# Issuing the small adapter loads of block 0 on two queues behind the first piece of x

## The chip, the cores and the metric

The kernel runs on one core of one Trainium2 chip. The metric is the device time of one execution in microseconds, a median over several runs.

## What is computed

The input x has 8 sequences of 256 tokens with 1024 features. Each sequence picks one of eight low-rank adapters (rank 16) by an id that is known only when the program runs. The adapted tokens go through a gated feed-forward layer with fp8 rounding of its inputs, and the result is added to x:

```python
Bx  = einsum('bni,bri->bnr', x, B[ids])          # B: 8 x 16 x 1024
h   = einsum('bnr,bor->bno', Bx, A[ids])         # A: 8 x 1024 x 16
gate, up = q(h / s_g) @ Wg.T, q(h / s_u) @ Wu.T  # 1024 -> 2752, q rounds to fp8
hid = silu(gate) * up
out = x + q(hid / s_d) @ Wd.T                    # 2752 -> 1024
```

## The kernel before

The 2048 tokens are four blocks of 512, of two sequences each, and the 2752 hidden features are 22 chunks of 128 (the last is half full). TensorE does everything in one long sequence whose order is written out by hand (`multiply`, L469, keeps program order; all its matmuls carry the line number L470). It starts with matmuls on zeros (`warm`, L633). Then, for block 0, come B (`two_times_b`, tile bx: eight steps over the features, k = 0 to 7), A (`two_times_a`, tile c, rounded to fp8 into xg), and the gate and up matmuls of the first five weight chunks (tile y). Blocks 1 to 3 take their turns among the first chunks. The other chunks follow for all blocks, and then the down projection (tile yd).

All loads go through queues of DMA transfers. Most are issued by SyncE (SP), one after the other in the order of the program. Two are issued by ScalarE (ACT): the ids, and one half of B. A load whose address depends on an id needs that id in a register of the issuing engine: `adapter_of` (L362) loads it there from the tile ids_i.

For block 0 the loads are these:

- x in three pieces, of which the first has k = 0 to 3 (1 MB), the second k = 4 to 6 (0.75 MB), the third k = 7 (0.25 MB); `load_x(0, 0)`, `load_x(0, 4)` and `load_x(0, 7)`.
- B for its two sequences (`load_b`, 68 KB each). B's tile also carries the scales. The k-th step of bx needs B and that k of x.
- A for its two sequences (`load_a_two`, two loads of 32 KB for each, into rows of a tile that POOL has set to zero, L357). The first matmul to tile c needs all four.
- the weights of the first five chunks (`load_gate_up`, 1 MB each; chunk 0 in two halves). The y matmuls need them in that order.

The scheduler gives each load one of eight landing semaphores, in turn and in the order of the program, and a load that reuses a semaphore is issued only after the earlier load on it has landed. In the kernel before, the turns are: ids, x's first piece, B and B, x's second piece, and three of the four A loads; then the fourth A load (waits for the ids), x's third piece (waits for x's first piece), chunk 0's halves (wait for the two B loads), chunk 1 (waits for x's second piece), and the others.

Of the kernel before, what the change touches and what calls it, by code (L numbers as in the profile page):

```python
# [59 lines left out]
def x_of(x4, t, k):  # L60

    first = 0
    for n in PIECES[t]:
        if k < first + n:
            break
        first += n
    at = (t * NH + first) * P * TB
    piece = x4[at : at + n * P * TB].rearrange("(p k n) -> p k n", p=P, k=n)
    return piece, first
# [214 lines left out]
def adaln_ffn(  # L284
# [13 lines left out]
    nc = tc.nc  # L298
# [38 lines left out]
    with ExitStack() as fast:  # L337
# [14 lines left out]
        b_two = [lora.tile([P, 2 * BROW + R], F32, name=f"b{t}") for t in range(2)]  # L352
# [9 lines left out]
        def adapter_of(batch, queue):  # L362
            return queue.value_load(ids_i[0:1, batch : batch + 1], min_val=0, max_val=7)  # L363

        def load_b(b, i, adapter, queue):
            queue.dma_start(  # L366
                out=b[:, i * BROW : (i + 1) * BROW], in_=b8[bass.ds(adapter * P, P), :]
            )

        def load_a_two(t, j, adapter):  # L370
            for g in range(2):
                row = 32 * (2 * g + j) + R * j
                nc.sync.dma_start(
                    out=a_two[t][row : row + R],
                    in_=a8[bass.ds(adapter * 2 * R + g * R, R), :],
                )

        def load_x(t, k):
            piece, first = x_of(x4, t, k)
            ks = slice(first, first + piece.shape[1])  # L380
            nc.sync.dma_start(out=xs[t][:, ks, :], in_=piece)
# [9 lines left out]
                nc.sync.dma_start(out=w[:, bass.ts(i, n)], in_=src[:, bass.ts(i, n)])  # L391
            w_of[c] = w

        load_x(0, 0)
        load_b(b_two[0], 0, adapter_of(0, nc.scalar), nc.scalar)
        second = adapter_of(1, nc.sync)
        load_b(b_two[0], 1, second, nc.sync)


        load_x(0, 4)  # L400
        load_a_two(0, 1, second)
        load_a_two(0, 0, adapter_of(0, nc.sync))
        load_x(0, 7)
        for c in range(NFIRST):
            load_gate_up(c, parts=1 if c else 2)
# [5 lines left out]
        for j in range(2):  # L411
            load_a_two(1, j, adapters.pop(0))
# [317 lines left out]
        for k in range(NH - 1):  # L730
# [23 lines left out]
            first = k % 2 == 0  # L754
# [29 lines left out]
    with found_others.Else():  # L784
# [11 lines left out]
        t, cols = NTB - 1, slice(cut, TB)  # L796
# [88 lines left out]
```

## Time and profile before

| what | value |
|---|---|
| median of 3 runs | 476.82 us (476.09 to 476.93) |
| the profiled execution | 477.12 us |
| its span, first to last instruction | 475.3 us |
| TensorE matmuls busy | 469.8 us, 99% of the span |
| granted TensorE clock | 1.0 |
| DMA, mean over the span | 112 GB/s |
| x's first piece, issue to landing | 5.0 us |
| the two halves of B, issue to landing | 3.2 and 3.3 us |
| x's third piece, issue to landing | 2.9 us |

Times in the views are counted from the span's first instruction. A line of the timeline gives start, length, engine, line of the kernel, operation, the tiles written and read, how many instructions were merged, and in brackets how long the engine was idle before it and what ended that. An engine's name with a q (SPq, ACTq) stands for what its queue issues. "DMA x<-x" in the chain is a transfer from its issue to its landing.

### The profile page before, as it was taken

What the parts mean: (1) busy time and instruction counts of PE and PEld (TensorE: products, weight loads), DVE (VectorE), ACT (ScalarE), POOL (GpSimd) and SP (SyncE); (2) the same over time, 40 slices, a digit from 0 to 9 for tenths busy, and PEclk for the clock granted to TensorE, in tenths of its full rate; (3) what the DMA queues carried; (4) which work ended last, traced back from release to release, by engine and by line L of the source; (5) the groups of instructions that cost most, each with busy time, mean ns of one, the idle gap of its engine ahead of it and who ended that gap; (6) DMA issues with size and microseconds to landing.
All of it is one profiled execution on the core that took longest, in us unless ns stands there. A gap on an engine that the chain in (4) does not pass through costs nothing.

```text
span 475.3 us, 6009 instructions
## 1 busy us (share of the span) xinstructions
PE 469.8 (99%) x2514; PEld 217.0 (46%) x2514; DVE 105.6 (22%) x163; ACT 192.5 (40%) x249; POOL 1.0 (0%) x7
## 2 busy tenths in 40 slices
PE   8999999999999999999999999999999999999997
PEld 4454544444444444444444444444444444444444
DVE  1333432121212222121212212132120121031031
ACT  1322447995556654533454554359212022021000
POOL 0000000000000000000000000000000000000000
PEclk9999999999999999999999999999999999999999
DMA  8995013422222112222211111123335255063031
GB/s 291 406 405 186 1 48 133 176 88 90 88 88 89 24 66 89 90 88 88 90 30 60 44 62 56 61 83 123 103 146 161 64 185 161 22 213 114 3 116 66
DMA packets 13780, 53.44 MB, mean 112 GB/s; under 512 B 1650, under 2 KB 2930, under 8 KB 10674
## 3 DMA queue, kind: packets, MB, share of 16 engines
q1 hardware_dynamic: 13600, 52.92, 32.1%
q8 instruction: 21, 0.34, 0.3%
q14 instruction: 13, 0.11, 0.1%
q10 hardware_dynamic: 146, 0.07, 0.0%
HBM read 44.60 MB, written 8.39 MB: 111 GB/s over the span
## 4 chain that ended last, share of the span: by engine, by line
PE 96%; DMA 3%; SPq 0%; issue 0%; DVE 0%
PE y L470 62%; PE yd L470 31%; DMA w_gu<-w_gu 2%; PE c L470 1%; PE bx L470 1%; DMA x<-x 1%; DMA ids_i<-ids 0%; SPq L363 0%; SPq L366 0%; DVE o L695 0%; PE count L470 0%
## 5 line engine op out<-in xcount | busy, mean ns | idle before, releaser
L470 PE MATMUL y<-xg,w_gu 128*128 128x512 fp8e4 x1376 | 298.4, 379 | 0.9 <-DMA w_gu<-w_gu 0.9
L470 PEld LDWEIGHTS <-w_gu 128*128 128x128 bf16 x1376 | 134.0, 98 | 163.8 <-DMA w_gu<-w_gu 1.8
L470 PE MATMUL yd<-hid,w_d 128*128 128x512 fp8e4 (+2 forms) x693 | 146.0, 373 | 0.0
L609 ACT ACTIVATE g<-y,gate_s 128x512 f32<-128x512 f32 (+1 forms) x88 | 59.8, 681 | 137.2 <-PE y L470 137.2
L610 DVE SCALAR_TENSOR_TENSOR hid<-y,up_by_down,g 128x512 fp8e4<-128x512 f32 x84 | 63.1, 751 | 220.3 <-PE y L470 162.2
L470 PEld LDWEIGHTS <-w_d 128*128 128x128 bf16 x693 | 66.6, 98 | 79.0 <-issue 1.7
L456 ACT ACTIVATE junk<-w_d 128x1408 bf16<-128x1408 uint16 (+1 forms) x16 | 21.2, 1324 | 88.4 <-DMA w_d<-w_d 88.3
L695 DVE SCALAR_TENSOR_TENSOR o<-yd,down_s,x 128x512 f32<-128x512 f32 x28 | 20.0, 748 | 107.4 <-PE yd L470 92.8
L456 ACT ACTIVATE junk<-w_gu 128x2048 bf16<-128x2048 uint16 (+1 forms) x22 | 41.0, 1863 | 0.0
L463 ACT ACTIVATE junk<-hid 128x2048 bf16<-128x2048 fp8e4 x21 | 40.0, 1905 | 0.4
L463 ACT ACTIVATE junk<-xg 128x2048 bf16<-128x2048 fp8e4 x8 | 15.3, 1909 | 0.3
L528 ACT ACTIVATE xg<-c,inv 128x512 fp8e4<-128x512 f32 x16 | 9.7, 688 | 8.6 <-PE c L470 8.6
L526 DVE TENSOR_SCALAR xg<-c,inv 128x512 fp8e4<-128x512 f32 x16 | 10.9, 744 | 2.8 <-PE c L470 2.8
L470 PE MATMUL warm<-zeros 128*128 128x512 bf16 (+1 forms) x27 | 6.5, 402 | 1.2 <-DVE zeros L309 1.2
L695 DVE SCALAR_TENSOR_TENSOR o<-yd,down_s,xg 128x512 f32<-128x512 f32 (+2 forms) x5 | 3.2, 644 | 12.3 <-PE yd L470 12.3
L516 ACT COPY bm<-bx 64x128 f32<-64x128 f32 x4 | 1.0, 262 | 9.7 <-PE bx L470 9.6
L470 PE MATMUL bx<-x,b 128*32 128x128 f32 x128 | 4.3, 276 | 0.6 <-DMA x<-x 0.6
L470 PEld LDWEIGHTS <-zeros 128*128 128x128 bf16 x27 | 2.6, 116 | 4.7 <-issue 3.0
L470 PE MATMUL c<-bm,a 32*128 32x128 f32 x128 | 4.3, 277 | 0.0
L456 ACT ACTIVATION_READ_ACCUMULATOR junk<-w_gu 128x1 f32 x22 | 4.2, 191 | 0.0
L470 PEld LDWEIGHTS c<-bm,a 32*128 32x128 f32 x128 | 3.9, 186 | 0.5 <-ACT bm L516 0.4
L470 PE MATMUL yd<-hid_tail,w_dt 64*128 64x512 bf16 (+1 forms) x32 | 4.1, 377 | 0.0
(47 smaller groups left out, 41.0 us busy)
## 6 DMA issues: line engine op xcount, KB each, us to landing
w_gu<-w_gu SPq DMA_DIRECT2D x20, 1024.0 KB, 4.8
outT<-o SPq DMA_DIRECT2D x31, 256.0 KB, 2.2
w_d<-w_d SPq DMA_DIRECT2D x8, 704.0 KB, 4.8
w_d<-w_d SPq DMA_DIRECT2D x8, 640.0 KB, 3.9
x<-x SPq DMA_DIRECT2D x2, 2048.0 KB, 11.1
x<-x SPq DMA_DIRECT2D x2, 1024.0 KB, 8.6
x<-x SPq DMA_DIRECT2D x2, 768.0 KB, 9.5
w_gu<-w_gu SPq DMA_DIRECT2D x3, 512.0 KB, 3.8
```

What stands on the lines that cost most here:

```text
L456: nc.scalar.activation(junk_like(w), low(w), AF.Copy, accum_out=lows[:rows, column : column + 1])
L463: nc.scalar.activation(junk_like(q), q, AF.Square, accum_out=squares[:rows, column : column + 1])
L470: tc.keep_in_program_order(nc.tensor.matmul(*args, **kwargs))
L516: copy(bm[64 * to : 64 * (to + 1), other], bx[half][64 * half : 64 * (half + 1)],)
L526: nc.vector.tensor_scalar(to, c, scale, None, ALU.mult, saturate=False)
L528: nc.scalar.activation(to, c, AF.Copy, scale=scale, saturate=False)
L609: nc.scalar.activation(g[rows], gates, AF.Silu, scale=gate_s[: gates.shape[0]])
L610: nc.vector.scalar_tensor_tensor(to, in0=ups, scalar=up_by_down[rows], in1=g[rows], op0=ALU.mult, op1=ALU.mult, saturate=False,)
L695: nc.vector.scalar_tensor_tensor(o, in0=y, scalar=down_s, in1=x, op0=ALU.mult, op1=ALU.add)
```

## The change

The four A loads of block 0 move ahead of x's second piece, and the two of the first sequence are issued by ACT, behind the half of B that ACT issues already. SP no longer loads the first sequence's id, since ACT has it in a register. The order on SP becomes: x's first piece, B, two A loads, x's second piece, x's third piece, weights. The order on ACT: ids, B, two A loads. In the turns of the semaphores the four A loads now come fifth to eighth, x's second piece reuses that of the ids, x's third piece that of x's first piece as before, and chunk 1 that of an A load.

```diff
-        def load_a_two(t, j, adapter):
+        def load_a_two(t, j, adapter, queue=nc.sync):
             for g in range(2):
                 row = 32 * (2 * g + j) + R * j
-                nc.sync.dma_start(
+                queue.dma_start(
                     out=a_two[t][row : row + R],
                     in_=a8[bass.ds(adapter * 2 * R + g * R, R), :],
                 )
...
         load_x(0, 0)
-        load_b(b_two[0], 0, adapter_of(0, nc.scalar), nc.scalar)
-        second = adapter_of(1, nc.sync)
+        first, second = adapter_of(0, nc.scalar), adapter_of(1, nc.sync)
+        load_b(b_two[0], 0, first, nc.scalar)
         load_b(b_two[0], 1, second, nc.sync)
-
-
+        load_a_two(0, 0, first, nc.scalar)
+        load_a_two(0, 1, second)
         load_x(0, 4)
-        load_a_two(0, 1, second)
-        load_a_two(0, 0, adapter_of(0, nc.sync))
         load_x(0, 7)
```

## The prediction on record

> **What bounds the kernel now.** I read the page first: busy shares, then the chain that ended last.
>
> ```profile
> PE 469.8 (99%) x2514; PEld 217.0 (46%) x2514; DVE 105.6 (22%) x163; ACT 192.5 (40%) x249; POOL 1.0 (0%) x7
> PE 96%; DMA 3%; SPq 0%; issue 0%; DVE 0%
> ```
>
> TensorE is the bound for 96% of the chain, and the change touches no matmul. Only the 3% under DMA can move. So I asked for the chain in order of time, to see where that part lies (start, length, what).
>
> ```profile
> 2.92 0.37 SPq L366
> 3.29 0.04 issue
> 3.33 4.97 DMA x<-x
> 8.30 0.02 issue
> 8.32 8.85 DMA w_gu<-w_gu
> 17.17 0.05 issue
> 17.21 13.12 PE y L470 x60
> ```
>
> The last DMA on the chain is the weights of chunk 1, landed at 17.17 us. From 17.21 on the chain holds nothing but TensorE up to the last eviction, so the kernel ends 458 us after that landing, whatever came before. The question is therefore one number: when does chunk 1 land? Third, the timeline of the first 18 us (start, length, instruction, idle before it).
>
> ```profile
> 2.88 0.41 ACTq L366 DMA_DIRECT2D b<-b  x1
> 2.92 0.37 SPq L366 DMA_DIRECT2D b<-b  x1
> 3.33 0.45 SPq L381 DMA_DIRECT2D x<-x  x1
> 4.00 2.58 SPq L373 DMA_DIRECT2D a<-a  x4
> 6.62 0.42 SPq L381 DMA_DIRECT2D x<-x  x1
> 7.09 2.99 SPq L391 DMA_DIRECT2D w_gu<-w_gu  x6
> 8.34 0.86 PE L470 MATMUL bx<-x,b 128*32 128x128 f32 x24 [0.22 <-DMA x<-x]
> 9.59 0.43 PE L470 MATMUL bx<-x,b 128*32 128x128 f32 x8 [0.38 <-DMA x<-x]
> 14.70 1.90 PE L470 MATMUL y<-xg,w_gu 128*128 128x512 fp8e4 x8 [0.23 <-DMA w_gu<-w_gu]
> 17.21 13.12 PE L470 MATMUL y<-xg,w_gu 128*128 128x512 fp8e4 x60 [0.62 <-DMA w_gu<-w_gu]
> ```
>
> SyncE (SP) spends 2.58 us on the four A loads, and x's third piece is issued only after them, at 6.62. TensorE waits four times for data, 0.22 + 0.38 + 0.23 + 0.62 = 1.45 us in all; 0.85 of it is for weights. Fourth, the DMA's rate in stretches (the last column is GB/s, the one before it the share of the 16 engines).
>
> ```profile
> 5.00:5.50 0.50, 0.50 (x3) 0.25 (x2) 0.00 (x0) 0.00 (x0) 0.00 (x0) 1.00 1.14 380
> 7.00:7.50 0.50, 0.50 (x29) 0.50 (x20) 0.00 (x0) 0.00 (x0) 0.00 (x0) 1.00 0.95 373
> 7.50:8.00 0.50, 0.50 (x16) 0.25 (x8) 0.00 (x0) 0.00 (x0) 0.00 (x0) 1.00 0.89 176
> 8.00:8.50 0.50, 0.28 (x11) 0.16 (x12) 0.00 (x0) 0.00 (x0) 0.00 (x0) 1.00 0.52 160
> 8.50:9.00 0.50, 0.50 (x24) 0.44 (x16) 0.00 (x0) 0.00 (x0) 0.00 (x0) 1.00 1.19 426
> ```
>
> Around 400 GB/s is normal here; between 7.5 and 8.5 the stream runs at 176 and 160. The loss is 0.5 x (1 - 176/400) + 0.5 x (1 - 160/400) = 0.58 us of transfer time. It is the stretch in which x's second piece is done and the third, issued at 6.62, has not begun to flow. I call it the hole.
>
> **What the Trainium skill says.** (1) "DMA: Bandwidth & Descriptors", section "Issuing engines are not separate DMA queues": loads from ACT and SP share the same 16 engines, and a second issuing queue saves only issue time. This decides what to count: not a second stream, but SP's 2.58 us. The trace agrees as far as it goes: B's two halves, issued at 2.88 on ACT and 2.92 on SP, took 3.2 and 3.3 us to land. (2) Same page, "Queues, rings and completion order": on each engine a queue's descriptors are consumed in ring order, and an engine drains a packet before it turns to another queue. The trace agrees: B on ACT's otherwise empty queue landed at 6.08, after x's first piece (issued 0.75, 5.0 us to landing, so 5.75). (3) Same page, "Latency and other measured facts": first byte about 0.6 us after the issue. Here the measurement decides: x's third piece was issued at 6.62, and the rate is back only after 8.1, so 1.5 us from issue to flow.
>
> **The change part by part.** Nothing is added or taken away in computing. One register load of batch 0's adapter (0.28 us with 0.16 us of register arithmetic behind it) goes from SP; ACT already holds that register.
>
> *ACT's side.* Two A loads follow B on ACT, at about 3.5 and 4.1 us by SP's pitch (4.00 to 4.59 for the first two A loads). ACT's next work is the copy at 10.11 us, which waits for TensorE until then: cost zero, and the cover is 5 us thick. Both A tiles' zeroing (0.53 us from 1.02 on POOL) is long done.
>
> *SP's side.* B ends at 3.29. Before, the first A came 0.22 us after its predecessor's end, so now at 3.51, the second 0.59 us later at 4.10, ending 4.43. x's second piece is issued at 4.47, 1.14 us later than the 3.33 of before. The third piece could go at 4.96, but in the compiled order it reuses the landing semaphore of x's first piece (eight in rotation), so it waits for 5.75 and goes at 5.77, 0.85 us earlier than 6.62. The weights follow at 6.24 instead of 7.09; their own semaphores belong to B (6.08 and 6.22) and to A, all landed by about 6.7. Queued behind that wait on SP are only weight loads, and the stream has x's second piece to move meanwhile.
>
> *The hole of before.* x's second piece, issued 4.47, flows from about 4.47 + 1.5 = 5.97. Its 0.79 MB take 1.97 us at 400 GB/s, to 7.94. The third piece is ready at 5.77 + 1.5 = 7.27: it follows without a gap. The hole closes: -0.58 us.
>
> *A new hole?* x's first piece landed at 5.75; its last byte moved earlier. x's third piece flowed from 8.1 for 0.65 us and landed at 9.52, 0.77 later; so the first was through between 5.0 and, with no such delay on most engines, 5.5. I take 5.25. B's 0.139 MB and A's 0.131 MB now lie between it and the second piece: 0.27/0.4 = 0.67 us, to 5.92. The second piece is ready at 5.97. Bounds: with 1.0 us to flow it is there at 5.47 and there is no hole; with 2.1 us, which would be the case if it behaves as B did (3.2 us to landing less some 1.1 for arriving), it is there at 6.57 and leaves 0.65 us. I take 1.5, as measured for the third piece of x, and 0.08 us for a ragged change. Net for the stream: 0.58 - 0.08 = 0.5 us earlier.
>
> *TensorE's side.* The first bx group starts at 6.71 behind the warm-up matmuls, which end at 6.78; x's first piece (5.75) and B (6.08, 6.22) have half a microsecond to spare, so it stays. x's second piece lands 0.35 us later (A is now ahead of it), 8.65 instead of 8.30, so the 24 matmuls run 8.65 to 9.51. The third piece lands at 7.94 + 1.3 = 9.2, in time; the last eight start at 9.51 instead of 9.59. Everything to the first y follows: 12.50 instead of 12.58. Two groups of eight (1.89 and 1.90) end at 16.29 if chunk 0's second half is there at 14.39; it lands at 14.65 - 0.5 = 14.15. Chunk 1 lands at 17.17 - 0.5 = 16.67, later than 16.29, so DMA still ends last and the whole 0.5 us counts. Late next would be TensorE itself at 16.29: a gain beyond 0.92 us is closed. After that, loads that came 0.5 us earlier meet a TensorE that is 0.5 us earlier too.
>
> Sum: the profiled execution goes from 475.3 to about 474.8 of span, 477.12 to about 476.6 with the 1.8 us around it. The median shown, 476.82, lies 0.3 below that execution; I apply the 0.5 to it: 476.3.
>
> **The rivals.** *The hole only moves* (18%). The second piece of x needs 2.1 us to flow, a hole of 0.65 at 6 us replaces that of 0.58 at 8 us: 476.82 + 0.07 = 476.9. For it: the second piece is issued 1.14 us later. Against it: 0.27 MB of B and A fill just that time.
>
> *The lag of the last share, longer: slower* (17%). Chunk 0's first half landed at 10.9 (7.09 + 3.8), its second only at 14.65, 3.75 us later, while the stream moved about 1.4 MB and the half has 0.52. At the rates there (336, then 397 GB/s) 1.4 us would do, so the last share of it came 2.3 us behind the rest, and chunk 1 behind it. Place: the first weights, 11 to 15 us, beside the fp32 matmuls. The two queues' small loads shift what meets there. Price: the lag's growth less 0.5, so it decides above 0.5 us of growth. Nothing shows its size; between no growth and doubling I take 1.5: 477.8. Against it: the same weights come in the same order.
>
> *The lag goes* (15%). Chunk 1 is then early, and TensorE's 16.29 is the limit: 0.92 us, 475.9.
>
> That the change does not do what it says is excluded: the compiled order has the loads so.
>
> **How the numbers follow.** The forecast has 50%, by itself 475.9 to 476.8. A difference of 0.2% (0.95 us) is about what a measurement of this kernel can tell; the three runs lie 0.84 us apart. Faster by that: about half of the vanished lag and a tenth of the forecast, 0.13. Slower: six tenths of the longer lag and a little of the moved hole, 0.13. Within: 0.74. The range, 475.6 to 477.7, leaves out half of the longer lag and a quarter of the vanished one.
>
> **What would show it.** Right: third piece of x issued near 5.8, weights near 6.2; no stretch under 300 GB/s between 7 and 9; second piece of x landed near 8.65; the y group behind chunk 1 starting near 16.7. Wrong: a stretch under 250 GB/s between 5.5 and 6.5 (the hole moved); chunk 1 later than 17.2 with the stream full (the lag); the first bx group later than 6.8 (B late); or a change after 20 us, where I expect none.

## The result, and the profile after

The changed kernel takes 478.04 us (median of 20 runs, 477.19 to 479.6), the kernel before 476.88 (median of 20, 475.71 to 478.39). The ratio is 1.0024, with a 95% interval of 1.0014 to 1.0035: slower by 0.24%, or 1.16 us. The forecast was 476.3, with a range up to 477.7. It failed in sign.

The runs of the changed kernel fall into two groups. In 11 of the 20 the mean granted TensorE clock is 0.999 or 1.0, and their median is 477.38. In the other 9 it is 0.996, and their median is 478.79. The profiled execution is one of the quick ones: 477.19 us, the least of the 20, with a span of 475.4. The profiled execution of before (477.12) was slower than its median. So the two spans, 475.3 and 475.4, hide the difference, and the stages have to be compared instead.

First the chain that ended last in the changed kernel, in order of time (start, length, what):

```profile
4.42 0.04 issue
4.47 5.68 DMA x<-x
10.14 0.04 issue
10.19 1.09 PE bx L470 x32
11.28 0.50 PE warm L470 x7
11.77 2.10 PE c L470 x63
13.88 16.52 PE y L470 x76
```

The weights are gone from the chain. The last data that anything waits for is x's second piece. It is issued at 4.47, as the prediction worked out, but lands at 10.15, not at 8.65. Everything after it is TensorE without a gap. The timeline of the same kernel shows the wait (in the brackets) and the issues:

```profile
3.48 0.95 ACTq L373 DMA_DIRECT2D a<-a  x2
3.52 0.91 SPq L373 DMA_DIRECT2D a<-a  x2
4.47 1.46 SPq L381 DMA_DIRECT2D x<-x  x2
6.12 3.11 SPq L391 DMA_DIRECT2D w_gu<-w_gu  x6
8.71 0.40 PE L470 MATMUL warm<-zeros 128*128 128x128 bf16 x4
10.19 1.09 PE L470 MATMUL bx<-x,b 128*32 128x128 f32 x32 [1.08 <-DMA x<-x]
13.83 16.56 PE L470 MATMUL y<-xg,w_gu 128*128 128x512 fp8e4 x76
```

TensorE's four waits of before are one now, 1.08 us long, and no y waits for weights. The first bx group starts at 7.70, for 6.71 before. The prediction named that as the sign of a late B, but B landed 3.2 and 3.3 us after its issue as before; here the warm-up matmuls took 6.57 us for 5.58. In a second profile of this kernel the group starts at 6.86 with the same landing of x, so the end does not hang on it. Last, the rate in the stretches of half a microsecond, with the same columns as before (the last two are the engines' share and GB/s):

```profile
5.50:6.00 0.50, 0.50 (x3) 0.22 (x2) 0.00 (x0) 0.00 (x0) 0.00 (x0) 1.00 1.20 270
6.00:6.50 0.50, 0.50 (x3) 0.16 (x2) 0.37 (x6) 0.00 (x0) 0.00 (x0) 1.00 1.09 147
6.50:7.00 0.50, 0.50 (x2) 0.15 (x1) 0.13 (x2) 0.00 (x0) 0.00 (x0) 1.00 0.18 61
7.00:7.50 0.50, 0.50 (x3) 0.13 (x1) 0.00 (x0) 0.00 (x0) 0.00 (x0) 1.00 1.15 418
7.50:8.00 0.50, 0.50 (x14) 0.31 (x16) 0.00 (x0) 0.00 (x0) 0.00 (x0) 1.00 1.11 393
8.00:8.50 0.50, 0.50 (x29) 0.50 (x20) 0.00 (x0) 0.00 (x0) 0.00 (x0) 1.00 0.87 356
```

The hole of before, at 7.5 to 8.5, is gone, but a deeper one has opened at 5.5 to 7.0. Against 400 GB/s it loses 0.5 x (130 + 253 + 339)/400 = 0.90 us, where the old one lost 0.58. These columns count a packet (the unit in which an engine moves data) where it starts. The trace's record of single packets says more. The second piece has 128 packets of 6 KB. The first starts at 5.94; the 18 that start before 6.5 take 0.76 us each on the average, where in the kernel before every one took 0.23. Spread over their duration, the packets keep the engines 0.68, 0.70 and 0.95 busy in the three rows from 5.5 to 7.0. So a part of the hole is engines without work, and the larger part is the first packets of the second piece, which crawl.

### The profile page after: what moved, and what is told of

It is laid out like the page before. It is cut to its first block, busy times and chain, and to the rows that moved or that the text cites. A ratio compares the mean times of both kernels' runs of the same rounds, so it can differ in the third digit from the quotient of the medians.

```text
span 475.4 us, 6006 instructions
## 1 busy us (share of the span) xinstructions
PE 470.2 (99%) x2514; PEld 217.4 (46%) x2514; DVE 105.6 (22%) x163; ACT 192.5 (40%) x249; POOL 1.0 (0%) x7
## 4 chain that ended last, share of the span: by engine, by line
PE 97%; DMA 1%; SPq 0%; issue 0%; DVE 0%
PE y L470 63%; PE yd L470 31%; PE c L470 2%; PE bx L470 1%; DMA x<-x 1%; DMA ids_i<-ids 0%; SPq L373 0%; SPq L363 0%; PE warm L470 0%; SPq L366 0%; DVE o L695 0%; PE count L470 0%
## 5 line engine op out<-in xcount | busy, mean ns | idle before, releaser
L526 DVE TENSOR_SCALAR xg<-c,inv 128x512 fp8e4<-128x512 f32 x16 | 10.9, 743 | 2.8 <-PE c L470 2.8
L470 PE MATMUL warm<-zeros 128*128 128x512 bf16 (+1 forms) x27 | 7.5, 447 | 1.2 <-DVE zeros L309 1.2
L516 ACT COPY bm<-bx 64x128 f32<-64x128 f32 x4 | 1.0, 262 | 10.9 <-PE bx L470 10.9
L470 PEld LDWEIGHTS bx<-x,b 128*32 128x32 f32 x128 | 3.2, 110 | 2.2 <-DMA x<-x 1.3
```

Of the source, the lines that this page charges most:

```text
L470: tc.keep_in_program_order(nc.tensor.matmul(*args, **kwargs))
L516: copy(bm[64 * to : 64 * (to + 1), other], bx[half][64 * half : 64 * (half + 1)],)
L526: nc.vector.tensor_scalar(to, c, scale, None, ALU.mult, saturate=False)
```

## Experiments

Two theories came out of the trace. *Late x*: x's second piece is issued too late, crawls at first, and holds TensorE. *Clock*: the long idle time that this leaves makes the TensorE clock drop in some executions, and that costs a further 1.4 us there. The rivals were that chance in the landing alone makes the spread, that A on a second queue is what hurts, and that the position of the load in its queue counts. The kernel before ran beside the experiments; its medians there lie between 476.57 and 477.05. So the ratios to it compare two experiments better than their times do.

**The changed kernel again** (no edit).

> The changed kernel once more. Theory 1 (clock): x's second piece lands near 10.1 us, TensorE stands idle for about 1 us before it, and in about half of the executions the clock then drops for one stretch; runs with a mean clock of 0.996 take 478.2 to 479.6, those with 1.0 take 477.2 to 478.1; median near 478.0. Theory 2 (late landing alone): the spread is that of the landing, and the clock has no part in it; then the times of runs with 0.996 and with 1.0 overlap.

Measured: 477.61 us, ratio 1.0023 (1.0011 to 1.0035). 4 of 14 runs have a clock of 0.996 and take 478.47 to 479.23; the other 10 take 477.13 to 477.81. The groups do not overlap, nor did those of the first 20 runs (477.19 to 478.11 and 478.19 to 479.6). Low clocks were fewer than half. In this profile the landing is the same (10.15), TensorE's idle time 1.92 us: its warm-up was over earlier.

**A filler in the idle time**, to test the clock.

```diff
-        bm = two_times_b(0, lambda k: pass_time(warm, 4) if k == 3 else None)
+        bm = two_times_b(0, lambda k: pass_time(warm, 36) if k == 3 else None)
```

> The changed kernel with 36 small matmuls on zeros, not 4, between the first half of bx and the second (about 2 us at full clock), so that TensorE is busy while x's second piece is awaited. Theory 1 (clock): no run with a mean clock below 0.998, median 477.3 to 477.8, up to 0.5 us of it the filler's own overhang. Theory 2 (late landing alone): median 478.0 or more, as the filler takes away no wait for data.

Measured: 477.51 us, ratio 1.0017 (1.001 to 1.0025), and no low clock in 19 runs, against 13 in the 34 runs of the changed kernel. The low clock goes with the idle time. The median hardly falls. A likely reason is the filler itself: behind a first bx group that ends as late as in the first profile (8.7), its 2.18 us would run to about 10.9, past the landing at 10.15. No profile here shows such an execution.

**Two queues alone**: A split over ACT and SP, x's second piece ahead of A as before.

```diff
+        load_x(0, 4)
         load_a_two(0, 0, first, nc.scalar)
         load_a_two(0, 1, second)
-        load_x(0, 4)
```

> One part of the change alone: two of the four A loads go to ACT, but x's second piece stays ahead of A on SP, as before. Both theories: the second piece is issued at 3.33 and lands near 8.3, the third is issued near 5.8 in place of 6.62, the stretch under 200 GB/s at 7.5 to 8.5 is gone. TensorE's long idle time is gone: 476.2 to 476.9, not slower than before. If moving A to ACT itself cost something, 477.5 or more.

Measured: 476.06 us, ratio 0.9984 (0.9977 to 0.999), faster than before, and no low clock in 22 runs. Its issues on SP and its rates where the old hole was:

```profile
3.34 0.46 SPq L381 DMA_DIRECT2D x<-x  x1
4.01 0.92 SPq L373 DMA_DIRECT2D a<-a  x2
5.76 0.36 SPq L381 DMA_DIRECT2D x<-x  x1
```

```profile
7.50:8.00 0.50, 0.50 (x28) 0.50 (x20) 0.00 (x0) 0.00 (x0) 0.00 (x0) 1.00 1.02 316
8.00:8.50 0.50, 0.50 (x16) 0.25 (x8) 0.00 (x0) 0.00 (x0) 0.00 (x0) 1.00 1.00 287
```

176 and 160 GB/s have become 316 and 287, with the third piece issued at 5.76; no y waits for weights. So half of the change does what the prediction said of the whole. The landing, 9.01, was later than the 8.3 expected.

**Order alone**: all of A ahead of x's second piece, on SP.

```diff
-        load_a_two(0, 0, first, nc.scalar)
         load_a_two(0, 1, second)
+        load_a_two(0, 0, adapter_of(0, nc.sync))
         load_x(0, 4)
```

> The other part alone: all four A loads ahead of x's second piece, all on SP, with SP's register load of the first id. The second piece is issued near 6.2, after SP's 2.6 us for A, and flows about 2.4 us later, at 8.6; it lands near 11.8. The end moves by 1.6 us against the changed kernel if TensorE's chain from that landing is all that counts: 478.8 to 480.5. If the landing were not what holds the changed kernel, 477 to 478.

Measured: 478.01 us, ratio 1.0026 (1.0015 to 1.0036); 2 of 11 runs at 0.996. The order by itself costs as much as the whole change. The size was missed. The piece was issued at 6.12, but landed at 10.41, 4.3 us later: a load issued 1.65 us after the changed kernel's landed only 0.26 us after it.

**A bridge**: x's third piece ahead of A, so that the engines have data until the second is ready, at the same issue time.

```diff
+        load_x(0, 7)
         load_a_two(0, 0, first, nc.scalar)
-        load_a_two(0, 1, second)
+        load_a_two(0, 1, second, nc.sync, (0,))
         load_x(0, 4)
-        load_x(0, 7)
+        load_a_two(0, 1, second, nc.sync, (1,))
```

> The changed kernel with x's third piece (0.25 MB) issued behind B on SP, ahead of the A loads, and one of SP's A loads behind x's second piece, so that the second piece is issued at the same time as in the changed kernel, about 4.4. Theory restart (the second piece meets engines that have run dry, and its first packets crawl for about 1 us): the third piece keeps the engines busy until the second is ready, no stretch under 250 GB/s between 5.5 and 7.5, the second piece lands at 8.8 to 9.2 in place of 10.15, and the time is 476.0 to 476.8 with no run at a clock of 0.996. Theory issue time (a later issue is a later landing by itself): landing at 10.0 to 10.2, time 477.2 to 478 as in the changed kernel.

Measured: 479.37 us, ratio 1.004 (1.003 to 1.0051). Both expectations failed: the second piece, issued at 4.39, landed at 10.85, and the rate stayed at 234 to 311 GB/s from 6.0 to 9.5. Empty engines alone are not why the piece is slow. But 13 of 19 runs had the low clock (479.46, against 477.86 for the others), and the profile caught one. Its TensorE timeline, and its clock (the third number from the end) by microsecond:

```profile
10.89 1.08 PE L471 MATMUL bx<-x,b 128*32 128x128 f32 x32 [2.61 <-DMA x<-x]
12.40 3.70 PE L471 MATMUL c<-bm,a 32*128 32x128 f32 x64
```

```profile
11.00:12.00 1.00, 1.00 (x34) 0.80 (x34) 0.00 (x0) 0.00 (x0) 0.00 (x0) 1.00 1.03 393
12.00:13.00 1.00, 1.00 (x17) 0.90 (x19) 0.57 (x2) 0.52 (x2) 0.00 (x0) 0.67 1.08 451
13.00:14.00 1.00, 1.00 (x26) 1.00 (x25) 0.00 (x0) 0.00 (x0) 0.00 (x0) 0.50 1.02 434
```

At 12.34, 1.45 us after the idle time of 2.61 us has ended, the clock goes to half, and the 64 matmuls to c take 3.70 us instead of 2.17.

**The bridge with a filler.**

```diff
-        bm = two_times_b(0, lambda k: pass_time(warm, 4) if k == 3 else None)
+        bm = two_times_b(0, lambda k: pass_time(warm, 46) if k == 3 else None)
```

> The bridge kernel, of whose runs 13 of 19 had a clock of 0.996 and took 1.6 us longer than the other 6, with 46 small matmuls on zeros in place of 4 before the second half of bx (2.6 us at full clock, about its idle time of 2.61). Theory clock: no run at 0.996, all between 477.6 and 478.6, median near 478.0 in place of 479.37. If the low clock has another cause than the idle time, about two thirds of the runs keep it, and the median stays above 479.

Measured: 477.88 us, ratio 1.0024 (1.0016 to 1.0033), no low clock in 12 runs, all within 477.51 to 478.34. Against the kernel before, 42 added matmuls of no use made the bridge kernel about 0.8 us faster (1.0024 for 1.004), and none of its runs was as slow as any low-clock run of the bridge (479.14 and more). With that the clock theory is shown for this place.

**One A pair ahead**, the other on SP behind x; nothing but B on ACT.

```diff
-        load_a_two(0, 0, first, nc.scalar)
         load_a_two(0, 1, second)
         load_x(0, 4)
         load_x(0, 7)
+        load_a_two(0, 0, adapter_of(0, nc.sync))
```

> The changed kernel without its second queue's A loads in front: x's second piece is issued at 4.46 as there, behind SP's two A loads, and the two others follow on SP behind x's third piece. If ACT's A loads beside SP's are what makes the second piece slow, it lands as before 5.0 us after its issue or sooner, at 9.0 to 9.5. If the late issue alone does it (theory lead), it lands at 10.0 to 10.4, and TensorE's idle time and the runs at 0.996 are as in the changed kernel. The weights are 1.2 us later on SP, which does not count as long as x's landing holds the end.

Measured: 477.57 us, ratio 1.002 (1.0011 to 1.0028), 6 of 21 runs at 0.996. From its chain:

```profile
4.45 5.56 DMA x<-x
10.02 0.04 issue
```

Issued at the same time as in the changed kernel, landed at nearly the same time (10.02 for 10.15), without A on ACT. The second queue is cleared.

**In between**: the second piece between SP's two A loads.

```diff
-        load_a_two(0, 1, second)
+        load_a_two(0, 1, second, nc.sync, (0,))
         load_x(0, 4)
+        load_a_two(0, 1, second, nc.sync, (1,))
```

> The changed kernel with x's second piece between SP's two A loads: issued at about 3.95, halfway between 3.34 (two queues, x first: landed at 9.01) and 4.46 (changed: landed at 10.15). Theory lead (a load that is issued less than about 2 us before the engines come to it starts with crawling packets): landing at 9.3 to 9.8, time 476.3 to 477.0, few or no runs at 0.996. Theory of a fixed later landing (1.14 us of later issue for 1.14 us of later landing, the rest chance): 9.6 as well, so this run tells the dose and not the theory; a time above 477.3 would speak against both.

Measured: 476.25 us, ratio 1.0003 (0.999 to 1.0015), 1 of 13 runs at 0.996. The piece is issued at 3.92, and TensorE hardly waits for it:

```profile
3.92 0.43 SPq L381 DMA_DIRECT2D x<-x  x1
```

```profile
8.69 1.20 PE L471 MATMUL bx<-x,b 128*32 128x128 f32 x32 [0.16 <-DMA x<-x]
```

In this profile it was better than either theory said: half a microsecond of issue time, 3.92 or 4.46, goes with about 1.5 us of landing. But the runs fall apart. Eight of the 13 take 475.97 to 476.29, the other five 477.04 to 478.77, about as long as the changed kernel. The profile is of one of the eight. The piece may still land late in the five; no profile shows one of them.

**The same, with a register load ahead of the piece** (one more `adapter_of(2, nc.sync)` in front of `load_x(0, 4)`), so that it is issued late without another load in front. In the changed kernel, the bridge and the kernel with one A pair the piece was also the fifth load on SP, and this tells the two apart.

> The kernel with x's second piece between SP's two A loads (issued at 3.92 as the fourth load on SP, landed near 8.65), with one more register load on SP ahead of that piece, which moves its issue to about 4.5, the time of the changed kernel, while it stays the fourth load on SP. Theory time (issued after about 4.0 it meets engines that are through with the first piece, and crawls): landing at 10.0 to 10.4, median 477.2 to 478.0, some runs at a clock of 0.996. Theory count (in the changed kernel, the bridge kernel and the kernel with one A pair it is the fifth load on SP, and the fifth waits for an earlier one to finish): landing at 9.0 to 9.4, median 476.1 to 476.8, no clock at 0.996.

Measured: 477.78 us, ratio 1.0031 (1.002 to 1.0042), 7 of 21 runs at a clock of 0.996 and 2 at 0.993; none was below 477.14. Issued at 4.52 as the fourth load, it landed at 10.28. The rates of this kernel:

```profile
5.50:6.00 0.50, 0.50 (x4) 0.19 (x2) 0.00 (x0) 0.00 (x0) 0.00 (x0) 1.00 0.97 243
6.00:6.50 0.50, 0.50 (x8) 0.14 (x10) 0.47 (x6) 0.00 (x0) 0.00 (x0) 1.00 1.01 160
6.50:7.00 0.50, 0.50 (x24) 0.50 (x22) 0.04 (x1) 0.00 (x0) 0.00 (x0) 1.00 0.62 172
```

and of the kernel in between, without the register load:

```profile
5.50:6.00 0.50, 0.50 (x3) 0.23 (x2) 0.00 (x0) 0.00 (x0) 0.00 (x0) 1.00 0.93 288
6.00:6.50 0.50, 0.50 (x4) 0.21 (x3) 0.41 (x6) 0.00 (x0) 0.00 (x0) 1.00 1.13 442
6.50:7.00 0.50, 0.50 (x4) 0.10 (x1) 0.09 (x2) 0.00 (x0) 0.00 (x0) 1.00 1.02 344
```

Nothing but the register load and its 0.6 us of SP's time lies between the two, and in the changed kernel and the one with one A pair an A load took that time instead. Lateness does it.

**Fifth, but early**: the kernel in between, with `load_x(0, 7)` moved up right behind `load_x(0, 0)`, ahead of the registers.

> The same kernel with x's third piece issued on SP right behind the first, before the ids are there (about 1.15), so that the second piece is the fifth load on SP, still issued at about 3.9. The third piece puts 0.65 us of data ahead of B, A and the second piece. Theory time: no crawl, landing near 9.0 to 9.3, median 476.0 to 476.8. Theory count: crawl, stretches under 300 GB/s between 6 and 8, landing at 10 or later, median 477.2 or more.

Measured: 476.83 us, ratio 1.0004 (0.9994 to 1.0013), 1 of 13 runs at 0.996. The piece was issued at 3.93 and landed at 9.74, later than the theory of time said, and the third piece in front pushed B back too (the first bx group waited 0.96 us for B). But no half microsecond between 5 and 9 was under 295 GB/s, and the time was far from the changed kernel's. The count is not the cause.

**All of A on ACT**, x's second piece ahead of it.

```diff
-        load_a_two(0, 0, first, nc.scalar)
-        load_a_two(0, 1, second)
         load_x(0, 4)
+        load_a_two(0, 0, first, nc.scalar)
+        load_a_two(0, 1, adapter_of(1, nc.scalar), nc.scalar)
         load_x(0, 7)
```

> x's second piece ahead of A as before, and all four A loads on ACT (which loads the second id too); SP has x, B, x, x, weights. Both theories: the stream has no hole, since the third piece waits for the first piece's landing at 5.75 only; 475.9 to 476.6, like the kernel with two A loads on each queue. If it is faster than that one by over 0.3 us, SP's remaining 0.9 us for A still counted.

Measured: 476.08 us, ratio 0.9975 (0.9964 to 0.9986), no low clock in 8 runs. With the kernel of the two queues alone it is the best of the study. Whether SP's last 0.9 us for A counted stays open: the medians are alike (476.08 and 476.06), the ratio is lower here (0.9975 for 0.9984), and the two intervals overlap.

**All of x first**, all of B and A on ACT.

```diff
-        first, second = adapter_of(0, nc.scalar), adapter_of(1, nc.sync)
+        first, second = adapter_of(0, nc.scalar), adapter_of(1, nc.scalar)
         load_b(b_two[0], 0, first, nc.scalar)
-        load_b(b_two[0], 1, second, nc.sync)
-        load_a_two(0, 0, first, nc.scalar)
-        load_a_two(0, 1, second)
+        load_b(b_two[0], 1, second, nc.scalar)
         load_x(0, 4)
         load_x(0, 7)
+        load_a_two(0, 0, first, nc.scalar)
+        load_a_two(0, 1, second, nc.scalar)
```

> All three pieces of x issued at once on SP (0.75 to 2.0), all of B and A on ACT. Theory restart: the engines never run dry before the weights, x's second piece lands by about 8, TensorE waits for no x at all and starts y near 12.0 to 12.5; 475.3 to 476.1. Rival: B, on its own queue beside a full ring of x, lands later than 7, the first bx group moves back, and the gain is lost: 476.5 to 478.

Measured: 478.31 us, ratio 1.0024 (1.0016 to 1.0031). The rival held, and by a little more than its 478. The chain says why:

```profile
3.47 5.08 DMA b<-b
8.56 0.02 issue
8.58 4.34 DMA a<-a
12.92 0.04 issue
12.96 2.05 PE c L470 x58
```

B, alone on ACT's queue, took 5.08 us to land beside a full queue of x, where it took 3.2 before; A is late in turn. A queue of its own is no right of way.

## Why the prediction was wrong

Its steps, in its order:

- *The bound is when chunk 1 lands.* True of the kernel before, no longer after. The wait that ends last moved from the weights to x's second piece, 10.15.
- *Issue times.* Right: 4.47 for x's second piece (worked out 4.47), 6.12 for the weights (6.24).
- *The hole of before closes, -0.58 us.* Right in mechanism, where x's second piece stays first. In the kernel of the two queues alone the loss at 7.5 to 8.5 falls to 0.25 us by the same sum, and the weights are issued 0.92 us earlier. The kernel gained 0.16% (0.1 to 0.23), which is 0.76 us of 476.72.
- *"A new hole?"* This is the step that failed. It took 1.5 us from issue to flow, measured at x's third piece, a load of 2 KB rows, and 2.1 as its worst case. First bytes do come after 1.5 us (5.94), but the rate is full only at 7.0, 2.5 us after the issue. What it put at nothing is the time in which the first packets crawl. The trace of before had a nearer row, of which the prediction used only the landing: x's first piece, the one other large load that meets empty engines. Issued at 0.75, it moves 180 and 115 GB/s in the half microseconds from 2.0 and 2.5, and is at full rate from 3.0, so 2.25 us. Its first 19 packets, of 8 KB, took 0.77 us each, and 0.31 later:

```profile
2.00:2.50 0.50, 0.50 (x3) 0.20 (x2) 0.00 (x0) 0.50 (x1) 0.00 (x0) 1.00 1.05 180
2.50:3.00 0.50, 0.50 (x3) 0.22 (x2) 0.00 (x0) 0.09 (x1) 0.00 (x0) 1.00 0.32 115
3.00:3.50 0.50, 0.50 (x3) 0.18 (x2) 0.00 (x0) 0.00 (x0) 0.00 (x0) 1.00 1.08 459
```

  The rival in which the hole moves had this mechanism, with a hole of 0.65. It measured 0.90.
- *The landing.* The hole is only half of the 1.5 us by which x's second piece missed its forecast (10.15 for 8.65): 0.90 less the 0.08 allowed. By 8.7 us the DMA had moved 2.10 MB, about as much as the first two pieces of x with B and A hold (2.11). But while 90% of the second piece's packets had started by 8.46, the last started at 9.56, and 2.70 MB had moved when the piece landed: later loads went ahead of its last share. In the kernel before, these were 7.05 and 7.40.
- *TensorE's side.* It let the landing be 0.35 us later. It was 1.85 later (10.15 for 8.30). The first y is 1.25 us later (13.83 for 12.58), since the gap before the last eight bx matmuls is gone. The 0.85 us of waits for weights behind it are gone too, which leaves about 0.4 us. The median of the 11 quick runs, 477.38, is 0.5 above the 476.88 of the kernel before.
- *What was not in the sum: the clock.* The wait that grew was priced as time lost once. In 13 of the 34 runs of the changed kernel it also cost a stretch at half clock, about 1.4 us (478.79 against 477.38). Of the 167 runs of the kernel before beside the experiments, 3 had it. 0.5 us for every run and 1.4 for 9 of 20 make 1.1 us on the average, and the means of the two kernels differ by 1.15.
- *The lag of the last share of the weights.* The forecast's slower case named it for chunk 0. There it played no part, as no y waits for weights. It came at x's second piece instead, where the forecast had none.

Two things stay open. Why a load issued at 4.4 to 4.5 crawls is not settled. Empty engines fit the kernel with one A pair and the late fourth load, but in the bridge kernel there was data in front and the piece was slower still. And the length of the idle time is not the whole condition of the clock. The kernel with all of x first stood idle for 2.53 us before the first bx group and had no low clock in 22 runs. The last section has a condition that fits all the profiles; no run tests it.

## What to carry to other kernels

Moving small loads ahead of a large one is priced by what the large one meets when it comes: look in the trace for a load of its size that started on empty engines, and count from issue to full rate, not to the first byte. A wait on TensorE has a second price, a dropped clock, which one profile may not show, so read the clock of every run. And split a change that does two things: here the second queue gave 0.16% and the order took it back, and more.

## What was not expected of the hardware

- The clock drop has a fixed length. In the late-fourth kernel's profile, after 2.56 us of idle time, the clock by microsecond from 11 to 15 is 0.65, 0.50, 0.50 and 0.64: at half clock that is 0.70 + 1 + 1 + 0.72 = 3.42 us.

```profile
11.00:12.00 1.00, 1.00 (x23) 0.80 (x15) 0.53 (x2) 0.47 (x2) 0.00 (x0) 0.65 1.01 373
12.00:13.00 1.00, 1.00 (x15) 0.80 (x17) 0.04 (x1) 0.05 (x1) 0.00 (x0) 0.50 1.07 410
13.00:14.00 1.00, 1.00 (x26) 1.00 (x24) 0.00 (x0) 0.00 (x0) 0.00 (x0) 0.50 1.01 422
14.00:15.00 1.00, 1.00 (x32) 1.00 (x28) 0.65 (x1) 0.69 (x2) 0.00 (x0) 0.64 1.03 434
```

  The Trainium skill, "TensorE: Matmul & The Clock Gate", Part 1, has TensorE's clock at half when idle and a free-running activity window of about 3.4 us. The length agrees. Its section on HAM oscillation puts the limit at gaps of over about 3.4 us; here the clock fell after gaps of 2.56 and 2.61 us, so a shorter gap is enough, and the measurement decides.
- The drops keep step with the clock's first rise. In the trace's clock record of the late-fourth kernel the clock becomes full at 4.48, during the warm-up, falls at 11.30 and is full again at 14.72; in the bridge's, at 5.51, 12.34 and 15.75. (The record begins with the first rise, so the views show 1.00 before it too; the weight loads of the warm-up are 0.43 us apart until then, and about 0.21 after.) In both that is 6.83 and 10.24 us after the first rise, two and three times 3.41. Cut all 14 profiles into stretches of 3.41 us from the first rise, and add up TensorE's idle time in each stretch. The two drops come at the end of stretches with 2.44 and 1.97 us of it. No other stretch has over 1.53. The 2.53 us of the kernel with all of x first fall on two stretches (1.19 and 1.35), and so do the 1.92 us of the changed kernel's second profile (0.64 and 1.28). As the first rise came anywhere from 3.93 to 7.19, the same wait can fall into one stretch or on two. That would explain why only a part of the runs drops. It is a fit to 14 profiles with two drops among them, not a test.
- The landing of x's second piece does not follow its issue evenly. Issued at 3.33 to 3.35 in three kernels, it lands at 8.30, 9.01 and 8.54; issued at 3.92 it is there for a matmul at 8.69; issued at 4.39, 4.45, 4.47 and 4.52 it lands at 10.85, 10.02, 10.15 and 10.28; issued at 6.12 it lands at 10.41. Apart from the changed kernel, which has two profiles with the same landing, each of these is one profile.
